# Layer 2's attention: how the mask reaches the transposed scores

## The chip, the cores and the metric

The kernel runs on one core of a Trainium2 chip. A core has a matrix engine (TensorE, "PE" in the profile, with its weight loads as "PEld"), a vector engine (VectorE, "DVE"), a scalar engine for functions such as the exponential (ScalarE, "ACT"), a general engine (GpSimd, "POOL") and a queue for transfers (SyncE, "SP"). Each works through its own queue in order, and they wait for one another by semaphores. Matrix products are written to PSUM, where the kernel keeps eight buffers (4, 3 and 1, by its pools) of 512 float32 numbers per partition, one bank each; everything else lies in SBUF.

The metric is the device time in microseconds of one execution.

## The reference

The program is four layers over `x` of shape (16, 128, 128), each with an attention or a product like one and a feed-forward part, both added through gates:

```python
x = x + tanh(g_xattn[2]) * _L2_xattn_ref(_layernorm(x), ctx, ctx, mask, Wq, bq, Wk, bk, Wv, bv, Wo, bo)
x = x + tanh(g_ffn[2]) * _L2_ffn_ref(...)
```

Layers 0, 1 and 3 have experts as feed-forward parts, layer 2 has slots. The attention of layer 2 has 16 heads of width 8 and one 128 by 128 mask for all sequences and heads:

```python
scores = einsum('bhqd,bhkd->bhqk', q, k) * scale
scores = where(mask == 0, -1e9, scores)
attn = softmax(scores, axis=-1)
out = einsum('bhqk,bhkd->bhqd', attn, v)
```

A query whose whole row of the mask is 0 gets equal weights over all keys.

## The kernel before

The 16 sequences are treated in four groups of four (`GB`), so a tile holds 128 partitions by 4 x 128 numbers, 512 in float32, which is one bank. For each group there is a chain: expert layer 1, attention of layer 2 (`attention_2(g)`), slots (`slots_2`), attention of layer 3 (`attention_3`), expert layer 3. The expert layers are one long generator, `experts()`, the stream: each of its steps is the products `pg` and `pu` (L452, L453), a function on ScalarE (L457), two products of elements on VectorE (`sg`, L458, and `h`, L464), the routing weight on GpSimd (`hw`, L473), and, two steps later (`LAG`), the product `acc` (L1128). `until(...)` at the end of the program draws the stream on as far as the next attention needs it, so that the stream's next group runs beside an attention.

The text is not the order of the engines' queues. When the program is built, a planner lays out one queue per engine by the place of the instructions in the text and by when their inputs are ready; `in_turn` adds edges that keep some of them in the written order. On the chip these queues are fixed.

`attention_2(g)` projects queries and keys with the heads laid out over partitions, then loops over the four sequences t of its group (L638 to L672). One iteration:

- Scores, queries on partitions: four banks `ps`, each started by a bfloat16 product of the identity with `mb`, a tile that holds -BIG (2 to the power 100) at masked places (L642), then 16 score products added (L647). L493, called at L650, takes the row maxima over the two heads of a half bank into `mp`.
- `mp` is transposed (L653) and added to the queries (L654): the product with the keys' tile `kTm` then gives scores less their maximum.
- Transposed scores, keys on partitions: again four banks, each started by a product with the identity, here of `mbT`, the mask transposed (L657), then 32 score products (L663).
- For i from 0 to 3: the exponential of bank i into an SBUF tile `pts` of 128 x 512 (L669, three buffers), and `weighted` (L495 to L503), which multiplies it with the values (L499) and with ones (L502) into `po`: weighted sums and sums of weights. These products stand in a fixed order.
- `over_weights`: reciprocal (L507) and product (L508) into `oT`.

The eight score banks of an iteration and `po` come from one pool of four buffers (`mm_tile`, and `acc_tile` while `side` is "m"). `attention_3(g)` has the same loop over pairs of sequences (L787 to L817) without any mask. `mask_i` is the mask loaded as integers; `maskf` is 0 at kept and -1 at masked places, and 0 all over in a row without a kept place; `someb` (0 or 1 for each query) takes out the queries of such a row. `LOWEST` is -3.0e38.

Of the kernel before, what the change touches and what calls it, by code (L numbers as in the profile page):

```python
# [10 lines left out]
F32 = mybir.dt.float32  # L11
BF16 = mybir.dt.bfloat16
I32 = mybir.dt.int32
AF = mybir.ActivationFunctionType
ALU = mybir.AluOpType
AX = mybir.AxisListType

P = 128
# [10 lines left out]
LOWEST = -3.0e38  # L29
BIG = 2.0**100  # L30
# [29 lines left out]
def flamingo(ctx, tc, x_in, ctx_in, mask_in, w1, w2, w3, wslot, wsmall, slots, cols_in, rows_in, consts_in,  # L60
             gu0, dn0, gu1, dn1, gu3, dn3, out):
    nc = tc.nc
    PSUM = bass.MemoryType.PSUM
    const = ctx.enter_context(tc.tile_pool(name="const", bufs=1))
# [23 lines left out]
    def mm_tile():  # L88
        return bank("mm")

    def tr_tile():
        return bank("tr")

    def acc_tile():
        return ps_acc.tile([P, CH], F32, tag="acc", name="acc") if side[0] != "m" else bank("po")

    def split(ap, n=GB):
        return ap.rearrange("p (t d) -> p t d", t=n)

    def bc(ap, axis, n):  # L100

        a = ap.unsqueeze(axis)
        shape = list(a.shape)
        shape[axis] = n
        return a.to_broadcast(shape)

    def mm(o, l, r, start=True, stop=True):
        nc.tensor.matmul(out=o, lhsT=l, rhs=r, start=start, stop=stop)  # L108
# [164 lines left out]
    def normed_T(g):  # L273
        xn = normed(g)
        return xn, transposed(xn, tag_of("xnT"), act, 2 if side[0] == "x" else 1)

    def add_gated(g, y, gate):
        nc.vector.scalar_tensor_tensor(X[g][:], y, gate, X[g][:], ALU.mult, ALU.add)

    def add_row(g, r):  # L280
        nc.gpsimd.tensor_tensor(X[g][:], X[g][:], bc(r[:], 1, GB), ALU.add)
# [9 lines left out]
    def keys_by_head(o, w, src, name, s):  # L291


        n = o.shape[2]
        p = mm_tile()
        mm(p[:, :n], w, src)
        for j in range(2):
            nc.vector.tensor_scalar(o[:, j, :], p[:, :n], con("hm")[:, j:j + 1], hcol[f"{name}{s}{j}"], ALU.mult, ALU.add)
# [140 lines left out]
    def in_turn(chain, ins):  # L439

        if chain:
            tc.add_manual_dep(ins.ins, chain[-1].name,
                              mybir.DependencyInfo(mybir.DependencyClass.NoSync, mybir.DependencyReason.DATA),
                              reason="in_turn")
        chain[:] = [ins.ins]
# [33 lines left out]
    def values(n, h0, nh, src, bias):  # L479

        o = vp[:, 0:n, 24:].rearrange("p t (h x) -> p t h x", h=NH)[:, :, h0:h0 + nh, 0:DK]
        shape = dict(t=n, h=nh)
        nc.vector.tensor_tensor(o, src.rearrange("p (t h d) -> p t h d", **shape),
                                bias.rearrange("p (t h d) -> p t h d", **shape), ALU.add)

    def value(rows, t, h):

        at = 24 + 32 * h - DK * (h % 4)
        return vp[rows, t, at:at + 32]

    def maxima(mp, i, src, n, k):

        nc.vector.tensor_reduce(mp[:, 0:n, 32 * i + 16:32 * i + 18], src, AX.X, ALU.max)  # L493

    def weighted(chain, heads, r, first, last):  # L495


        for po, jj, vcols, pts, rows in heads:
            in_turn(chain, nc.tensor.matmul(out=po[32 * jj:32 * jj + 32, 0, :], lhsT=vcols, rhs=pts, start=first, stop=last,  # L499
                                     skip_group_check=True))  # L500
        for po, jj, vcols, pts, rows in heads:
            in_turn(chain, nc.tensor.matmul(out=po[32 * jj:32 * jj + 32, 1, :], lhsT=own[rows, r, :], rhs=pts, start=False,  # L502
                                     stop=last, skip_group_check=True))  # L503

    def over_weights(o, po, n):
        rc = work.tile([P, P], F32, tag="rcw", name="rcw")
        nc.vector.reciprocal(rc[:, :n], po[:, 1, :])  # L507
        nc.vector.tensor_tensor(o, po[:, 0, :], rc[:, :n], ALU.mult)  # L508
# [113 lines left out]
    def attention_2(g):  # L622
        _, xnT = normed_T(g)
        add_row(g, ob2)
        qT = act.tile([P, 2, GT], F32, tag="qT", name="qT2")
        kTm = act.tile([P, 2, 2, GT], F32, tag="kTm", name="kTm2", bufs=1)
        for s in range(2):
            p = mm_tile()
            mm(p[:], W2H[:, s, :], xnT[:])
            nc.vector.scalar_tensor_tensor(split(qT[:, s, :]), split(p), hcol[f"bq2{s}"], bc(someb[:], 1, GB),  # L630
                                           ALU.add, ALU.mult)
            keys_by_head(kTm[:, s], W2H[:, 2 + s, :], CT[g][:], "bk2", s)
        pv = mm_tile()
        for t in range(GB):
            mm(pv[:, t * P:(t + 1) * P], CT[g][:, t * P:(t + 1) * P], w(W2, 0))
        values(GB, 0, NH, pv[:], bvr)
        oT = act.tile([P, GT], F32, tag="oT", name="oT2")
        for t in range(GB):  # L638
            b = slice(t * P, (t + 1) * P)
            ps = [mm_tile() for _ in range(4)]  # L640
            for i in range(4):
                nc.tensor.matmul(out=split(ps[i]), lhsT=identb[:], rhs=bc(mb[:], 1, 4), start=True, stop=False,  # L642
                                 skip_group_check=True)
            for s in range(2):
                for i in range(4):
                    rr = slice(32 * i, 32 * i + 32)
                    nc.tensor.matmul(out=split(ps[i])[:, 2 * s:2 * s + 2, :], lhsT=qT[rr, s, b], rhs=kTm[rr, s, :, b],  # L647
                                     start=False, stop=True, skip_group_check=True)
            for i in range(4):
                maxima(mp[:, 2 * t:2 * t + 2], i, ps[i][:].rearrange("p (s j k) -> p s j k", s=2, j=2), 2, P)  # L650
            pt = tr_tile()
            for s in range(2):
                nc.tensor.transpose(pt[:, s * P:(s + 1) * P], mp[:, 2 * t + s, :], ident[:])  # L653
            nc.vector.tensor_tensor(qT[:, :, b], pt[:, 0:2 * P].rearrange("p (s q) -> p s q", s=2), qT[:, :, b], ALU.add)  # L654
            ps = [mm_tile() for _ in range(4)]
            for i in range(4):
                nc.tensor.matmul(out=split(ps[i]), lhsT=identb[:], rhs=bc(mbT[:], 1, 4), start=True, stop=False,  # L657
                                 skip_group_check=True)
            for s in range(2):
                for j in range(2):  # L660
                    for i in range(4):
                        rr = slice(32 * i, 32 * i + 32)
                        nc.tensor.matmul(out=split(ps[i])[:, 2 * s + j, :], lhsT=kTm[rr, s, j, b], rhs=qT[rr, s, b],  # L663
                                         start=False, stop=True, skip_group_check=True)
            po = acc_tile()[:, 0:2 * P].rearrange("p (i q) -> p i q", i=2)
            chain = []
            for i in range(4):
                pts = work.tile([P, 4, P], F32, tag="pts", name="pts", bufs=3)
                nc.scalar.activation(pts[:], split(ps[i]), AF.Exp, scale=scale8)  # L669
                weighted(chain, [(po, jj, value(slice(0, P), t, 4 * jj + i), pts[:, jj, :], slice(0, P)) for jj in range(4)],  # L670
                         i, i == 0, i == 3)
            over_weights(oT[:, b], po, P)  # L672
        py = split(mm_tile())
        for t in range(GB):
            mm(py[:, t, :], oT[:, t * P:(t + 1) * P], w(W2, 1))
        add_gated(g, py, tgx[:, 2:3])
# [617 lines left out]
    pp = tr_tile()  # L1294
# [22 lines left out]
    pp = tr_tile()  # L1317
# [2 lines left out]
    nc.vector.tensor_copy(someb[:], pp[:, 0:P])  # L1320
    pp = tr_tile()
    nc.tensor.transpose(pp[:, 0:P], maskf[:], ident[:])
    mbT = const.tile([P, P], BF16, tag="mbT", name="mbT")
    nc.vector.tensor_scalar(mbT[:], pp[:, 0:P], BIG, None, ALU.mult)
    mb = const.tile([P, P], BF16, tag="mb", name="mb")
    nc.vector.tensor_scalar(mb[:], maskf[:], BIG, None, ALU.mult)
    identb = const.tile([P, P], BF16, tag="identb", name="identb")
# [11 lines left out]
    pp = mm_tile()  # L1339
# [3 lines left out]
    pp = mm_tile()  # L1343
# [3 lines left out]
    pp = tr_tile()  # L1347
# [3 lines left out]
    pp = mm_tile()  # L1351
# [24 lines left out]
    for g in range(NG + 1):  # L1376
        if g < NG:
            until(1, g)
            attention_2(g)
        if g > 0:  # L1380
            until("slots", g - 1)
            attention_3(g - 1)
# [78 lines left out]
```

## Time and profile before

Three runs took 898.25, 898.9 and 900.76 us: a median of 898.9.

| what | value |
|---|---|
| the profiled execution | 897.76 us |
| its span, first to last instruction | 896.1 us |
| granted TensorE clock, mean | 0.978 |
| products with `mbT` (L657) | 64, median 379 ns each |
| score products behind them (L663) | 512 instructions, median 270 ns |
| exponentials (L669) | 64, median 597 ns |
| maxima (L493) | 112, median 682 ns |
| `hw` on GpSimd (L473) | 142, median 1268 ns |

A busy time is the sum of the instructions' own times with overlaps taken once. TensorE's instructions are pipelined: one that is listed with 379 ns has its successor start long before it ends, so the cost of one in a row of many is the distance between starts. The iterations of `attention_2` lie in four stretches of the span, about 279 to 326, 351 to 402, 483 to 534 and 607 to 659 us, one for each group.

### The profile page before, as it was taken

Reading aid. Unit: us, or ns where it says so; the run is one execution under the profiler, and the core shown is the slowest. Engines: PE = TensorE matmul, PEld = TensorE weight load, DVE = VectorE, ACT = ScalarE, POOL = GpSimd, SP = SyncE. Lnnn points to the kernel's source line nnn. Section 1 sums busy time; section 2 is a strip of 40 time slices with the busy share of each in tenths; the row PEclk is TensorE's granted clock in tenths of the full one; section 3 lists DMA queues with packets and bytes.
Section 4 is the critical chain, followed back from the end, with each engine's and each line's share of the span. In section 5 each row is a group of like instructions: output and inputs, shape, how many; then the busy total and the mean of one; then the engine's idle time right before and its main releaser. Section 6 shows DMA issues by size and latency. Waiting matters only on the chain.

```text
span 896.1 us, 16095 instructions
## 1 busy us (share of the span) xinstructions
PE 824.0 (92%) x6189; PEld 465.0 (52%) x6189; DVE 570.6 (64%) x1600; ACT 262.6 (29%) x472; POOL 298.9 (33%) x310
## 2 busy tenths in 40 slices
PE   5899599888988999998999989999999999999997
PEld 4554499444444544554555554555555544554443
DVE  5774433467888467468677666768666678667522
ACT  2522255232331221322222222232222232222321
POOL 4447421576452122114321115311133122313443
PEclk9899599999999999999999999999999999999999
DMA  9451122741321011011111203110002111211230
GB/s 296 143 129 35 59 63 78 218 146 35 96 68 39 26 37 47 25 25 60 48 48 47 60 27 125 65 38 25 25 16 82 49 36 49 72 49 60 86 115 27
DMA packets 55677, 62.12 MB, mean 69 GB/s; under 512 B 14312, under 2 KB 33512, under 8 KB 55472
## 3 DMA queue, kind: packets, MB, share of 16 engines
q1 hardware_dynamic: 53536, 57.67, 21.1%
q0 software_dynamic: 1536, 3.15, 1.2%
q8 instruction: 49, 0.80, 0.4%
q10 hardware_dynamic: 528, 0.26, 0.1%
q14 instruction: 28, 0.23, 0.1%
HBM read 53.97 MB, written 7.09 MB: 68 GB/s over the span
## 4 chain that ended last, share of the span: by engine, by line
PE 49%; DVE 21%; POOL 11%; issue 10%; DMA 5%; ACT 3%; SPq 1%; POOLq 0%; DVEq 0%; ACTq 0%
PE mm L108 7%; POOL hw L473 6%; PE acc L1128 6%; PE pu L453 6%; PE pg L452 5%; PE po L499 3%; DVE h L464 3%; DVE sg L458 3%; DVE mp L493 3%; PE mm L647 2%; POOL xd L974 2%; PE po L502 2%; POOL rs L259 2%; PE pg L1069 2%; DMA cb<-combD 2%
## 5 line engine op out<-in xcount | busy, mean ns | idle before, releaser
L473 POOL TENSOR_TENSOR hw<-h,cb 128x512 f32<-128x512 f32 (+1 forms) x142 | 175.4, 1235 | 441.9 <-DVE h L464 357.8
L453 PE MATMUL pu<-xnTx,wall 128*128 128x512 f32 x288 | 152.0, 610 | 6.6 <-DVE sg L458 3.7
L452 PE MATMUL pg<-xnTx,wall 128*128 128x512 f32 x288 | 151.8, 609 | 1.1 <-ACT xnTx L243 0.7
L1128 PE MATMUL acc<-hw,wall 128*128 128x512 f32 x288 | 151.0, 608 | 0.6 <-POOL hw L473 0.5
L464 DVE TENSOR_TENSOR h<-sg,pu 128x512 f32<-128x512 f32 x147 | 100.7, 685 | 71.4 <-PE pu L453 58.9
L457 ACT ACTIVATE sg<-pg 128x512 f32<-128x512 f32 x105 | 62.8, 598 | 221.5 <-PE pg L452 219.9
L458 DVE SCALAR_TENSOR_TENSOR sg<-sg,pg 128x512 f32<-128x512 f32 x105 | 71.4, 680 | 32.8 <-ACT sg L457 32.7
L453 PEld LDWEIGHTS pu<-xnTx,wall 128*128 128x128 f32 x288 | 51.2, 190 | 65.8 <-issue 44.8
L1128 PEld LDWEIGHTS acc<-hw,wall 128*128 128x128 f32 x288 | 53.1, 193 | 56.2 <-issue 48.6
L493 DVE TENSOR_REDUCE mp<-mm 128x4 f32<-128x512 f32 (+1 forms) x112 | 65.8, 646 | 21.1 <-PE mm L647 19.9
L452 PEld LDWEIGHTS pg<-xnTx,wall 128*128 128x128 f32 x288 | 49.6, 192 | 40.6 <-issue 30.0
L507 DVE RECIPROCAL rcw<-po 128x128 f32<-128x128 f32 (+1 forms) x28 | 25.2, 900 | 52.8 <-PE po L502 45.0
L460 ACT ACTIVATE sg<-pg 128x512 f32<-128x512 f32 x51 | 30.4, 596 | 81.5 <-PE pg L452 81.4
L499 PE MATMUL po<-pts,vp 128*32 128x128 f32 (+1 forms) x896 | 45.9, 273 | 6.0 <-ACT pts L669 5.5
L259 POOL TENSOR_TENSOR rs<-ve,neghalf 128x4 f32<-128x4 f32 x32 | 32.8, 1025 | 55.6 <-DVE ve L257 53.5
L270 DVE TENSOR_SCALAR xn<-x,mv,rs 128x128 f32<-128x128 f32 x104 | 36.7, 410 | 20.9 <-POOL rs L259 20.9
L669 ACT ACTIVATE pts<-mm 128x512 f32<-128x512 f32 x64 | 33.8, 600 | 54.8 <-PE mm L663 54.4
L502 PE MATMUL po<-pts,own 128*32 128x128 f32 (+1 forms) x896 | 44.2, 265 | 0.0
L499 PEld LDWEIGHTS po<-pts,vp 128*32 128x32 f32 (+1 forms) x896 | 21.6, 108 | 28.8 <-ACT pts L669 14.3
L251 DVE BATCH_NORM_STATS2 st<-x 128x6 f32<-128x128 f32 x128 | 31.1, 305 | 8.3 <-DMA x<-in_x 7.7
L241 PE MATMUL tr<-ident,xn 128*128 128x128 f32 x100 | 23.1, 314 | 13.1 <-DVE xn L270 11.7
L647 PE MATMUL mm<-kTm,qT 32*128 32x256 f32 x256 | 30.4, 413 | 0.0
(355 smaller groups left out, 1234.9 us busy)
## 6 DMA issues: line engine op xcount, KB each, us to landing
cb<-combD SPq DMA_DIRECT2D x72, 256.0 KB, 3.3
cb<-combD SPq DMA_DIRECT2D x128, 128.0 KB, 2.8
wall<-in_gu SPq DMA_DIRECT2D x24, 256.0 KB, 4.4
wall<-in_dn SPq DMA_DIRECT2D x12, 256.0 KB, 5.5
xb<-xd SPq DMA_DIRECT2D x7, 256.0 KB, 3.1
yd<-yb SPq DMA_DIRECT2D x7, 256.0 KB, 2.3
xd<-vp SPq DMA_DIRECT2D x1, 1072.0 KB
x<-in_x SPq DMA_DIRECT2D x4, 256.0 KB, 4.9
```

What stands on the lines that cost most here:

```text
L108: nc.tensor.matmul(out=o, lhsT=l, rhs=r, start=start, stop=stop)
L259: latest["rs"] = nc.gpsimd.tensor_tensor(rs[:], ve[:], neghalf[:], ALU.pow).ins
L452: in_turn(chain, nc.tensor.matmul(out=pg[:], lhsT=w[:, 0], rhs=xnT[:], start=True, stop=True))
L453: in_turn(chain, nc.tensor.matmul(out=pu[:], lhsT=w[:, 1], rhs=xnT[:], start=True, stop=True))
L457: nc.scalar.activation(sg[:], pg[:], AF.Tanh, scale=0.5)
L458: nc.vector.scalar_tensor_tensor(sg[:], sg[:], 1.0, pg[:], ALU.add, ALU.mult)
L464: ins = nc.vector.tensor_tensor(h[:], sg[:], pu[:], ALU.mult)
L473: latest["hw"] = nc.gpsimd.tensor_tensor(hw[:, at:], h[:, at:], cb[:, at:], ALU.mult).ins
L493: nc.vector.tensor_reduce(mp[:, 0:n, 32 * i + 16:32 * i + 18], src, AX.X, ALU.max)
L499: in_turn(chain, nc.tensor.matmul(out=po[32 * jj:32 * jj + 32, 0, :], lhsT=vcols, rhs=pts, start=first, stop=last, skip_group_check=True))
L502: in_turn(chain, nc.tensor.matmul(out=po[32 * jj:32 * jj + 32, 1, :], lhsT=own[rows, r, :], rhs=pts, start=False, stop=last, skip_group_ch ...
L1128: in_turn(chain, nc.tensor.matmul(out=acc[0][:], lhsT=w[:, 2], rhs=h[:], start=n == 0, stop=last))
```

## The change

The transposed scores get no product with the mask any more: the score products L663 start their banks themselves. The mask comes in behind the exponential. A tile `keptT`, the transposed mask plus one, is 1 at kept and 0 at masked places, in float32. One instruction on VectorE per bank takes the smaller of the exponential and 3.0e38, since the exponential of a masked score, whose maximum was taken over kept places alone, may be infinite, and multiplies it with `keptT`, repeated over the four heads of the bank, in place. The first scores (L642) keep their products with `mb`.

```diff
             ps = [mm_tile() for _ in range(4)]
-            for i in range(4):
-                nc.tensor.matmul(out=split(ps[i]), lhsT=identb[:], rhs=bc(mbT[:], 1, 4), start=True, stop=False,
-                                 skip_group_check=True)
             for s in range(2):
                 for j in range(2):
                     for i in range(4):
                         rr = slice(32 * i, 32 * i + 32)
                         nc.tensor.matmul(out=split(ps[i])[:, 2 * s + j, :], lhsT=kTm[rr, s, j, b], rhs=qT[rr, s, b],
-                                         start=False, stop=True, skip_group_check=True)
+                                         start=True, stop=True)
...
                 pts = work.tile([P, 4, P], F32, tag="pts", name="pts", bufs=3)
+
                 nc.scalar.activation(pts[:], split(ps[i]), AF.Exp, scale=scale8)
+                nc.vector.scalar_tensor_tensor(pts[:], pts[:], -LOWEST, bc(keptT[:], 1, 4), ALU.min, ALU.mult)
                 weighted(chain, [(po, jj, value(slice(0, P), t, 4 * jj + i), pts[:, jj, :], slice(0, P)) for jj in range(4)],
                          i, i == 0, i == 3)
...
-    mbT = const.tile([P, P], BF16, tag="mbT", name="mbT")
-    nc.vector.tensor_scalar(mbT[:], pp[:, 0:P], BIG, None, ALU.mult)
+    keptT = const.tile([P, P], F32, tag="keptT", name="keptT")
+    nc.vector.tensor_scalar(keptT[:], pp[:, 0:P], 1.0, None, ALU.add)
```

## The prediction

> **What bounds the kernel now.** I read the page's busy row, then the chain that ended last, then the time line of layer 2's attention. The page first:
>
> ```profile
> PE 824.0 (92%) x6189; PEld 465.0 (52%) x6189; DVE 570.6 (64%) x1600; ACT 262.6 (29%) x472; POOL 298.9 (33%) x310
> ...
> PE 49%; DVE 21%; POOL 11%; issue 10%; DMA 5%; ACT 3%; SPq 1%; POOLq 0%; DVEq 0%; ACTq 0%
> ```
>
> TensorE is nearly full over the whole span, but the chain lies on it for only half of the time: at many places TensorE waits for VectorE. So the question is what the four stretches of layer 2's attention wait for. Their busy times (columns: stretch, length, then busy us and count of PE, PEld, DVE, ACT, POOL, and clock, DMA):
>
> ```profile
> 279.00:326.00 47.00, 44.75 (x530) 24.17 (x530) 27.95 (x57) 12.26 (x22) 7.39 (x6) 1.00 0.09 28
> 351.00:402.00 51.00, 48.63 (x557) 27.57 (x556) 28.81 (x66) 16.18 (x28) 5.12 (x5) 1.00 0.08 24
> 483.00:534.00 51.00, 47.52 (x566) 27.95 (x565) 34.98 (x109) 12.99 (x24) 6.27 (x6) 1.00 0.14 43
> 607.00:659.00 52.00, 48.78 (x564) 28.40 (x563) 34.82 (x108) 12.98 (x24) 6.28 (x6) 0.97 0.08 26
> ```
>
> Each holds four iterations over t, 10.5 us apart in group 0 (the reciprocals of L507 start at 292.52, 303.03, 313.55) and 11 to 12 us later on. One iteration, from the time line (start, length, engine, line, operation, count, idle before):
>
> ```profile
> 297.48 0.44 PE L653 MATMUL tr<-ident,mp 128*128 128x128 f32 x2 [0.26 <-DVE mp L493]
> ...
> 297.76 1.06 PE L657 MATMUL mm<-mbT,identb 128*128 128x512 bf16 x4
> 297.96 0.42 DVE L654 TENSOR_TENSOR qT<-tr,qT 128x256 f32<-128x256 f32 x1 [0.53 <-PE tr L653]
> ...
> 298.74 1.17 PE L663 MATMUL mm<-qT,kTm 32*128 32x128 f32 x32
> ...
> 299.99 2.28 ACT L669 ACTIVATE pts<-mm 128x512 f32<-128x512 f32 x4 [2.13 <-PE mm L663]
> ...
> 301.01 0.69 DVE L464 TENSOR_TENSOR h<-sg,pu 128x512 f32<-128x512 f32 x1 [2.03 <-PE pu L453]
> ...
> 301.77 1.28 POOL L473 TENSOR_TENSOR hw<-h,cb 128x512 f32<-128x512 f32 x1 [9.24 <-DVE h L464]
> ...
> 302.56 0.40 PE L502 MATMUL po<-pts,own 128*32 128x128 f32 x8
> ...
> 303.03 0.96 DVE L507 RECIPROCAL rcw<-po 128x128 f32<-128x128 f32 x1 [1.34 <-PE po L502]
> ```
>
> It is one serial chain: maxima, transposes (L653), q (L654), transposed scores (L663), exponentials (L669), weighted values (L499, L502), reciprocal, next scores. Four score banks plus `po` share four buffers, so the next iteration can't run far ahead. The expert stream fills TensorE's waits with only some three pieces (pg, pu, acc) per iteration: 5 `h` lie in group 0's stretch, 4 in each of the others. So what lengthens this chain lengthens the program, unless more expert pieces move in.
>
> **Part 1, the 64 products of L657 go.** Three of them take 0.81 us with the last one's 0.38 in it, so one starts every 0.215 us: 4 per iteration are 0.86 us of TensorE, 64 are 13.8 us. That is the ceiling. What of it lies on the chain? In six iterations (like the one above) the four stand together and partly cover the wait for q: L653 to L663 takes 1.26 us; without them q is ready 0.90 us after L653 starts (297.48 to 298.38), and L663 would start at about 0.97. Worth 0.29. In the other ten an expert piece stands between them:
>
> ```profile
> 490.13 0.44 PE L653 MATMUL tr<-ident,mp 128*128 128x128 f32 x2
> 490.40 0.81 PE L657 MATMUL mm<-mbT,identb 128*128 128x512 bf16 x3
> ...
> 491.05 1.02 PE L1128 MATMUL acc<-hw,wall 128*128 128x512 f32 x2
> ...
> 491.91 0.38 PE L657 MATMUL mm<-mbT,identb 128*128 128x512 bf16 x1
> ...
> 492.22 1.17 PE L663 MATMUL mm<-qT,kTm 32*128 32x128 f32 x32
> ```
>
> Here it takes 2.09. Layer 3's attention has the same loop without mask products, and shows what stays with one expert piece in the gap:
>
> ```profile
> 459.95 0.38 PE L799 MATMUL tr<-ident,mp 128*128 128x128 f32 x2
> 460.17 1.02 PE L452 MATMUL pg<-xnTx,wall 128*128 128x512 f32 x2
> ...
> 461.12 1.17 PE L808 MATMUL mm<-qT,kTm 32*128 32x128 f32 x32
> ```
>
> 1.17 to 1.23 us there (two places), so 0.88 is gained. Sum: 10 x 0.88 + 6 x 0.29 = 10.5 us off the chain.
>
> **Part 2, 64 multiplications on VectorE come in,** each between an exponential and its eight value products. Nearest rows for 128x512 f32: `sm<-se,rsum` (L380), both inputs in SBUF, 688 ns; `sg` (L458), the same opcode, 680 ns. I take 0.69. Back to back they start closer: four maxima of 0.68 take 2.48 us, so 0.60 apart, which the exponentials (0.56 apart) just keep up with. From the first exponential's start to the reciprocal it is 3.04 us now (299.99 to 303.03), 0.76 of it behind the last exponential. Then: 0.60 for the first exponential, 0.05 for the signal, 3 x 0.60 + 0.69 for the train, 0.76 behind it: 3.90, so 0.86 more. 16 x 0.86 = 13.8 us onto the chain. VectorE's load grows by 64 x 0.69 = 44 us, 11 us per stretch. Queued behind a waiting multiplication are the expert stream's sg and h, and TensorE's acc and GpSimd's hw wait for those; acc runs two expert steps behind (LAG), which covers one such delay.
>
> **Part 3, what else stands in VectorE's queue.** An `h` lies at 301.01, exactly inside the coming train; in groups 2 and 3 the slot routing and the expert routing (109 instructions instead of 57) lie there. Ends: nothing, if all of it goes before or after the train, and 0.60 in each of 16 iterations, 9.6 us, if one does not. Half, 4.8 us.
>
> **Part 4, the port.** The row: a multiply-add with its tensors all in SBUF,
>
> ```profile
> L1098 DVE SCALAR_TENSOR_TENSOR x<-y,by,x x24: 321/346/2027, 171.4 to 251.1; 128x128 f32<-128x128 f32 x24
> ```
>
> has a median of 346 ns, a maximum of 2027 and a mean of 503: some waited for over a microsecond. `sg` and `h`, which read one input from PSUM, show no such tail (means 680 and 685). The Trainium skill, page "SBUF — State Buffer", section "Who interferes with whom", says why this speaks against the change: a VectorE instruction with two SBUF inputs and a GpSimd one that reads SBUF exclude each other for the whole instruction. By that rule each iteration's hw (1.27 us, at 301.77 inside the coming train) costs up to 1.27: 16 x 1.27 = 20 us. By the row it is less: the mean wait was 503 - 346 = 0.16 us where GpSimd was busy 58.8 of 103 us (stretch 176 to 279); in attention's stretches it is busy 25 of 201. Scaled by that, 0.16 x 0.125 / 0.57 x 64 = 2.2 us. I take the row, 2.5 us; both ends (0 and 20) stay for the range.
>
> **Part 5, filling.** The wait for the first weights grows from 0.76 us to 1.34 (0.60 + 0.05 + 0.69), and six gaps at q have room for a piece of 0.86 at 0.23 of cost: 6 x 0.63 = 3.8 us of expert work comes inside. I take 4 off. That more comes in is the first rival. The mask tile itself is made once, one 128x128 instruction for another (0.28 us, L1324) far ahead of its use: nothing, or 0.3 us if that cover is gone.
>
> **Sum.** -10.5 + 13.8 + 4.8 + 2.5 - 4 = +6.6 us. The profiled execution took 897.8 us with a span of 896.1; the median of the runs is 898.9. All differences are made in the span; set on the median, 905.
>
> **The rivals.** *TensorE stays the bound (faster).* 92% busy speaks for it: all 13.8 us return, the next iteration's mask and score products (0.2 us pieces) fill the gaps between the value products, expert pieces the rest. If 16 x 0.35 us stays unfilled: -13.8 + 5.6 = -8, about 891. Against it: the stream now places one expert step per iteration although room for more was there. *VectorE becomes the bound (slower by much).* Groups 2 and 3 go from 35 to 46 us busy of 51. The densest long stretch before reached 79.0 of 103, or 77%. At that share the four stretches need 50.5, 51.5, 59.7 and 59.5 us where they have 47, 51, 51 and 52: +20, about 919. It decides once slot and routing instructions can't move out into the stretches between. *The two chains cancel.* 10.5 or 13.8 against 13.8 with queue and port hidden: 896 to 902.
>
> **Chances and range.** A measurement of this kernel can tell about 0.3%, 2.7 us, from no change. Forecast (902 to 912) 0.45; VectorE the bound 0.18; cancelled 0.13; TensorE the bound 0.24. So faster 0.24, same 0.13, slower 0.63. The range goes from the faster rival's centre to near the slow one's: 889 to 919; the likeliest case's own range is 901 to 912.
>
> **What would show it.** L657 gone and L653 to L663 at 1.0 to 1.25 us everywhere (part 1). The first exponential to the reciprocal at 3.9 us or more against 3.04 (part 2). Multiplications with a median of 690 ns and a tail over 1.2 us beside hw (part 4). TensorE's busy time down by about the 18 us that its row for L657 holds, its idle time up by more than its work went down. I am wrong if the iterations come closer than 10.5 us apart, or if more than 5 `h` lie in one stretch: then the stream filled what I call idle.

## The result and the profile after

The changed kernel takes 910.7 us (908.0 to 914.1) where the kernel before takes 898.9: a ratio of 1.0135, interval 1.0113 to 1.0157. It is 12 us slower; the forecast was 905, or 6 us slower. The profiled execution took 910.67 us, 12.9 more than the one before.

The page of the changed kernel, first its span and busy times, then from its groups of instructions the value products (L499), the new multiplications (L668) and the exponentials (now L667); behind the bar of each group stand its busy us, the mean ns of one, and the idle time just before it with what ended it:

```profile
span 908.9 us, 16012 instructions
...
PE 821.5 (90%) x6125; PEld 459.9 (51%) x6125; DVE 615.3 (68%) x1664; ACT 263.0 (29%) x472; POOL 300.6 (33%) x310
...
L499 PE MATMUL po<-pts,vp 128*32 128x128 f32 (+1 forms) x896 | 47.6, 283 | 19.0 <-DVE pts L668 18.5
...
L668 DVE SCALAR_TENSOR_TENSOR pts<-pts,keptT 128x512 f32<-128x512 f32 x64 | 45.9, 757 | 8.5 <-ACT pts L667 8.4
...
L667 ACT ACTIVATE pts<-mm 128x512 f32<-128x512 f32 x64 | 34.7, 596 | 36.2 <-PE mm L660 19.7 <-PE po L502 13.1 <-DVE pts L668 3.4
```

The rows of the value products and of the exponentials in the kernel before:

```profile
L499 PE MATMUL po<-pts,vp 128*32 128x128 f32 (+1 forms) x896 | 45.9, 273 | 6.0 <-ACT pts L669 5.5
...
L669 ACT ACTIVATE pts<-mm 128x512 f32<-128x512 f32 x64 | 33.8, 600 | 54.8 <-PE mm L663 54.4
```

TensorE has 64 products less, yet its busy time fell by only 2.5 us, and its idle time (span less busy) rose from 72.1 to 87.4. It now waits 19.0 us ahead of the value products, for VectorE, where the row before had 6.0, for ScalarE. VectorE has 44.7 us more. The last row after holds what the forecast did not have: exponentials waited 13.1 us for L502, the products that read an earlier exponential.

One iteration of group 0 after, from the time line, to be held against 299.99 to 303.03 of the kernel before:

```profile
285.65 1.17 PE L660 MATMUL mm<-qT,kTm 32*128 32x128 f32 x32
...
286.90 1.57 ACT L667 ACTIVATE pts<-mm 128x512 f32<-128x512 f32 x3 [0.55 <-PE mm L660]
287.53 1.90 DVE L668 SCALAR_TENSOR_TENSOR pts<-pts,keptT 128x512 f32<-128x512 f32 x3 [0.29 <-ACT pts L667]
...
288.99 0.60 ACT L667 ACTIVATE pts<-mm 128x512 f32<-128x512 f32 x1 [0.51 <-PE po L502]
...
289.94 0.68 DVE L668 SCALAR_TENSOR_TENSOR pts<-pts,keptT 128x512 f32<-128x512 f32 x1
...
291.52 0.96 DVE L507 RECIPROCAL rcw<-po 128x128 f32<-128x128 f32 x1 [0.89 <-PE po L502]
```

Three exponentials go out at once. The fourth starts only at 288.99, after L502 has read the first tile: `pts` has three buffers, and a tile is now held for a multiplication longer. From the first exponential to the reciprocal it is 4.62 us; before it was 3.04, and the forecast said 3.90.

The four stretches, as before by stretch, length, busy us of PE, PEld, DVE, ACT, POOL, then the clock and DMA:

```profile
275.00:329.00 54.00, 49.24 (x534) 25.58 (x533) 41.74 (x79) 12.89 (x24) 9.40 (x7) 1.00 0.10 33
354.00:408.00 54.00, 49.04 (x540) 27.08 (x539) 42.47 (x112) 17.12 (x29) 9.13 (x10) 1.00 0.10 30
484.00:545.00 61.00, 53.40 (x556) 29.43 (x554) 49.74 (x130) 15.14 (x28) 8.80 (x8) 0.94 0.15 40
616.00:676.00 60.00, 52.69 (x554) 29.70 (x553) 49.48 (x128) 14.87 (x27) 8.42 (x8) 0.94 0.07 19
```

VectorE is busy over 80% of the last two, and the granted clock there is 0.94. For comparisons I set the borders of a stretch alike in every kernel, from the first L642 of a group to the end of its last `oT`. All sums of this kind below are mine, from the profiled executions:

| kernel | four stretches | TensorE idle in them | `h` in them | the rest of the span |
|---|---|---|---|---|
| before | 195.3 | 11.3 | 17 | 700.8 |
| after | 227.4 | 24.6 | 22 | 681.5 |

The stretches grew by 32.1 us, and the rest of the span fell by 19.3: five more expert steps, and other work of routing and slots, now run inside the stretches. That is the whole difference of 12.8.

### The profile page after: what moved, and what is told of

Its sections match the earlier page's. It is cut to its first block, busy times and chain, and to the rows that moved or that the text cites. A ratio compares the mean times of both kernels' runs of the same rounds, so it can differ in the third digit from the quotient of the medians.

```text
span 908.9 us, 16012 instructions
## 1 busy us (share of the span) xinstructions
PE 821.5 (90%) x6125; PEld 459.9 (51%) x6125; DVE 615.3 (68%) x1664; ACT 263.0 (29%) x472; POOL 300.6 (33%) x310
## 5 line engine op out<-in xcount | busy, mean ns | idle before, releaser
L499 PE MATMUL po<-pts,vp 128*32 128x128 f32 (+1 forms) x896 | 47.6, 283 | 19.0 <-DVE pts L668 18.5
L668 DVE SCALAR_TENSOR_TENSOR pts<-pts,keptT 128x512 f32<-128x512 f32 x64 | 45.9, 757 | 8.5 <-ACT pts L667 8.4
L259 POOL TENSOR_TENSOR rs<-ve,neghalf 128x4 f32<-128x4 f32 x32 | 32.8, 1026 | 52.9 <-DVE ve L257 50.5
L499 PEld LDWEIGHTS po<-pts,vp 128*32 128x32 f32 (+1 forms) x896 | 21.4, 111 | 56.7 <-DVE pts L668 41.2
L270 DVE TENSOR_SCALAR xn<-x,mv,rs 128x128 f32<-128x128 f32 x104 | 34.7, 390 | 21.0 <-POOL rs L259 21.0
L507 DVE RECIPROCAL rcw<-po 128x128 f32<-128x128 f32 (+1 forms) x28 | 25.2, 900 | 32.2 <-PE po L502 22.8
L502 PE MATMUL po<-pts,own 128*32 128x128 f32 (+1 forms) x896 | 46.4, 276 | 0.6 <-issue 0.6
L667 ACT ACTIVATE pts<-mm 128x512 f32<-128x512 f32 x64 | 34.7, 596 | 36.2 <-PE mm L660 19.7
```

The costliest lines, as they stand in the source:

```text
L270: nc.vector.tensor_scalar(xn[:, t, :], x[:, t, :], mv[:, t, 0:1], rs[:, t:t + 1], ALU.subtract, ALU.mult)
L668: nc.vector.scalar_tensor_tensor(pts[:], pts[:], -LOWEST, bc(keptT[:], 1, 4), ALU.min, ALU.mult)
```

## The experiments

My theory: what costs is the longer chain from exponential to reciprocal, made of the train of multiplications, the ring of three `pts` tiles, and VectorE's queue and port; what the planner moves into the longer stretches gives a part back. The rivals: VectorE's load as such, and the port alone.

**The two halves of the change.** One kernel has neither products nor multiplications (it leaves out the mask of the transposed scores), the other has both. The first edit is shown against the changed kernel, the second against the kernel before:

```diff
-                nc.vector.scalar_tensor_tensor(pts[:], pts[:], -LOWEST, bc(keptT[:], 1, 4), ALU.min, ALU.mult)
```

> Leaves out the mask of the transposed scores altogether: neither the 64 products nor the 64 multiplications, so that masked keys get weight. What the removal alone gives. The forecast's part 1 (the gaps before the transposed scores shrink from 2.09 and 1.26 us): 10.5 us off 898.9, about 888. TensorE is the bound everywhere: all 13.8 us off, 885. The products were covered by other waits: within 2 us of 899.

```diff
+                nc.vector.scalar_tensor_tensor(pts[:], pts[:], -LOWEST, bc(keptT[:], 1, 4), ALU.min, ALU.mult)
...
+    keptT = const.tile([P, P], F32, tag="keptT", name="keptT")
+    nc.vector.tensor_scalar(keptT[:], pp[:, 0:P], 1.0, None, ALU.add)
```

> The kernel before with the 64 multiplications added behind the exponentials and the 64 products kept: what the addition alone costs. The trace of the changed kernel shows 4.6 to 4.9 us from the first exponential to the reciprocal in group 0 where it was 3.04, so if the chain sets the time: 16 x 1.6 = 26 us less a little that the expert stream fills, about 921. If the multiplications only matter as load of VectorE, and the products went for nothing: 911, as the changed kernel.

Without any: 891.4 us, ratio 0.9923 (0.9895 to 0.9951), so the removal alone is worth 4 to 9 us. With both: 913.9, ratio 1.0167 (1.0143 to 1.0190): the addition alone costs 13 to 17. The two add up to +0.9% (-0.8% and +1.7%), less than the +1.35% measured, though their intervals together reach it. The gain is neither nothing nor all 13.8 us of products. In the kernel without mask, group 2's first gap shows why:

```profile
485.07 0.44 PE L653 MATMUL tr<-ident,mp 128*128 128x128 f32 x2
485.35 1.02 PE L1126 MATMUL acc<-hw,wall 128*128 128x512 f32 x2
486.21 0.27 PE L241 MATMUL tr<-ident,xn 128*128 128x128 f32 x1
486.73 1.17 PE L660 MATMUL mm<-qT,kTm 32*128 32x128 f32 x32 [0.24 <-DVE qT L654]
```

It takes 1.66 us in place of 2.09, not 1.20: the scores now wait for q on VectorE, which the products had covered. Over 16 iterations the gap fell from 1.77 to 1.40 on average, 5.9 us.

**A fourth tile in the ring,** in both kernels. There was no room for it, so the reciprocal's two buffers became one, and one small tile (two in the changed kernel) took the place of a dead one; two controls have that room alone. The other users of this tile's place, layer 3's attention among them, have four as well.

```diff
-                pts = work.tile([P, 4, P], F32, tag="pts", name="pts", bufs=3)
+                pts = work.tile([P, 4, P], F32, tag="pts", name="pts", bufs=4)
...
-        rc = work.tile([P, P], F32, tag="rcw", name="rcw")
+        rc = work.tile([P, P], F32, tag="rcw", name="rcw", bufs=1)
```

> The changed kernel with four buffers for the exponentials in place of three (the room comes from tiles that are no longer in use and from one buffer less for the reciprocal). Theory of the ring: the fourth exponential now waits for the value products of the first bank, which wait for the first multiplication; without that wait the stretch from the first exponential to the reciprocal falls from 4.7 to the forecast's 3.9 us, 16 x 0.75 = 12 us off, 899 to 902. Theory of load (VectorE has 44 us more to do and is what sets the time): no change, 909 to 912.

> Control: the kernel before with the same four buffers and the same room made. There the fourth exponential started 1.7 us behind the first with no wait, so both theories expect no change: 897 to 901.

> Control: the changed kernel with three buffers, and only the room made as for four (one reciprocal buffer, two tiles in the place of others). If that room has no price: 909 to 912. If it is what cost the kernel before 6 us: 916, and the fourth buffer then gained 6.

> Control: the kernel before with three buffers and the room made. If the room has no price: 898 to 900, and the 6 us of the run with four buffers come from the fourth buffer's order of work and the clock (granted 0.969 there, 0.978 before). If it has: 905.

Changed kernel with four: 910.2, ratio 1.0123 (1.0101 to 1.0146); with the room alone: 913.4, ratio 1.0150 (1.0124 to 1.0176). Kernel before with four: 905.4 (1.0069); with the room alone: 905.7 (1.0076). So the room is what cost the kernel before its 6 us, and the fourth tile did nothing for its time. (The expectation was wrong that nothing waited there: in group 0 the fourth exponential starts 1.68 us behind the first with three tiles and 1.45 with four.) In the changed kernel it gained some 3 us, with intervals that overlap, and not the 12 that I expected. Yet the wait itself went, as the time line of the changed kernel with four tiles shows:

```profile
287.70 2.06 ACT L667 ACTIVATE pts<-mm 128x512 f32<-128x512 f32 x4 [0.49 <-PE mm L660]
288.33 2.50 DVE L668 SCALAR_TENSOR_TENSOR pts<-pts,keptT 128x512 f32<-128x512 f32 x4 [0.23 <-ACT pts L667]
...
291.59 0.96 DVE L507 RECIPROCAL rcw<-po 128x128 f32<-128x128 f32 x1 [0.17 <-PE po L502]
```

All four go at once, and the reciprocal comes 3.89 us after the first exponential: the forecast's 3.90, which had been worked out without the ring. Over all sixteen iterations the time from exponential to reciprocal fell from 90.3 us (room alone) to 82.2, and the gaps before the scores fell by 2.5. Yet the stretches fell only from 225.6 to 223.1 us, and the rest of the span grew by 1.8. What was gained in the chain was lost again elsewhere in the iterations, and the clock may be part of it: inside the four stretches TensorE had half clock for 20.5 us with four tiles and for 10.2 with the room alone, which by an estimate (half of the difference) is up to 5 us. So the 3 us are what the fourth tile brought, and not the price of the ring by itself. That freeing the ring alone returns the loss is refuted.

**Exponentials in PSUM.** This takes ring and port away together: the exponential goes back into its score bank, and the multiplication has one input in SBUF.

```diff
-                nc.scalar.activation(pts[:], split(ps[i]), AF.Exp, scale=scale8)
-                nc.vector.scalar_tensor_tensor(pts[:], pts[:], -LOWEST, bc(keptT[:], 1, 4), ALU.min, ALU.mult)
+                nc.scalar.activation(split(ps[i]), split(ps[i]), AF.Exp, scale=scale8)
+                nc.vector.scalar_tensor_tensor(pts[:], split(ps[i]), -LOWEST, bc(keptT[:], 1, 4), ALU.min, ALU.mult)
```

> The changed kernel, but the exponential is written back into its score bank in PSUM, and the multiplication reads it there and writes the SBUF tile. The multiplication then has one input in SBUF, and the fourth exponential needs no free SBUF tile. Theory of ring and port: first exponential to reciprocal 3.9 us in group 0, multiplications at 690 ns with no tail (mean 757 in the changed kernel), 16 x 0.75 + 4 = up to 16 us off the chain, 900 to 906. Theory of load (VectorE's 44 us more): no change, 909 to 912. A price against it: banks come free one multiplication later, which could cost the next iteration's scores up to 0.7 us each, then 911 or more.

> As the run with exponentials in PSUM, with four SBUF tiles as well. Ring: nothing is left to gain by the fourth tile there, so as that run within 3 us, unless four tiles carry a price of their own, as the kernel before showed with them (905.4 for 899.1): then 6 us above it.

897.6 us, ratio 0.9982 (0.9970 to 0.9995): the whole loss is gone, with the same 64 multiplications on VectorE. In group 0 all four exponentials go at once, and the reciprocal comes 4.00 us after the first:

```profile
289.78 2.05 ACT L667 ACTIVATE mm<-mm 128x512 f32<-128x512 f32 x4 [0.54 <-PE mm L660]
...
293.78 0.96 DVE L507 RECIPROCAL rcw<-po 128x128 f32<-128x128 f32 x1 [0.31 <-PE po L502]
```

The stretches take 215.5 us and hold 22 `h` as the changed kernel's do, and the rest of the span is 680.4, near the 681.5 there. So the 12 us came out of the stretches, and they lie in the chain: from exponential to reciprocal the sixteen iterations take 80.7 us in all, 12.7 less than the changed kernel's 93.4. Of these, 3.3 us lie in the first iteration of group 1 (7.32 us there, 4.00 here), where the queue of ScalarE in the changed kernel has two loads of function tables between the third and the fourth exponential; here they stand behind the fourth. With four tiles too: 899.4 (1.0009), nothing more to gain. VectorE's 44 us of load as such can't be what makes the changed kernel slower than this one: they are all still there. Against the kernel without any mask (ratio 0.9923) the multiplications still cost some 5 us.

**The port alone.** Exponentials in SBUF and three tiles, but the second input in PSUM (the mask is left out, and the larger of exponential and score is taken):

```diff
-                nc.vector.scalar_tensor_tensor(pts[:], pts[:], -LOWEST, bc(keptT[:], 1, 4), ALU.min, ALU.mult)
+                nc.vector.scalar_tensor_tensor(pts[:], pts[:], -LOWEST, split(ps[i]), ALU.min, ALU.max)
```

> The changed kernel with the exponentials in SBUF and three buffers as there, but the second input of the instruction behind each exponential is the score bank in PSUM in place of the mask tile, and the larger of the two is taken: the mask is left out, and the weights are others. What it tells is the port alone: one input in SBUF, while the ring of three stays. If the port is most of the 13 us that exponentials in PSUM gave back: 899 to 903, and no instruction of it above 0.7 us. If the ring is: 908 to 911, with 4.6 us from the first exponential to the reciprocal in group 0. If each does half, 904 to 907.

The instruction by its line, min, median and max in ns, in the changed kernel and then in this one:

```profile
L668 DVE SCALAR_TENSOR_TENSOR pts<-pts,keptT x64: 675/684/1616, 287.5 to 671.6; 128x512 f32<-128x512 f32 x64
```

```profile
L668 DVE SCALAR_TENSOR_TENSOR pts<-pts,mm x64: 677/681/690, 289.3 to 671.0; 128x512 f32<-128x512 f32 x64
```

The tail is gone and the time is not: 911.0, ratio 1.0150 (1.0129 to 1.0171). Taking the port away brought nothing here. It did not come quite alone, though: in group 0 the time from exponential to reciprocal is now 4.5 to 5.8 us, and not the expected 4.6. The ring alone gave 3 us and the port alone none, yet the kernel without both is 13 us faster; that each hides behind the other fits this, but I have not shown it. Exponentials in PSUM change the planner's order too, as the table loads show, and what that is worth was not tested.

**Mixtures.** Multiplications from PSUM for the first banks, products for the last ones:

```diff
-            for i in range(4):
+            for i in range(2, 4):
...
+                to = split(ps[i]) if i < 2 else pts[:]
+                nc.scalar.activation(to, split(ps[i]), AF.Exp, scale=scale8)
+                if i < 2:
+                    nc.vector.scalar_tensor_tensor(pts[:], to, -LOWEST, bc(keptT[:], 1, 4), ALU.min, ALU.mult)
```

> A mixture: banks 0 and 1 masked by multiplications read from PSUM, banks 2 and 3 by products with the identity as before. By the chain: first exponential to reciprocal 3.1 us (as before, since the last banks' exponentials set it), two products of 0.43 us in the wait for q, most of it covered: 891 to 895, below both kernels. By TensorE's work: 6.9 us less than before, the same range. By VectorE's load (22 us more): 905.

> As the mixture, with only bank 3 masked by a product: first exponential to reciprocal 3.4 us, three multiplications per iteration. By the chain 893 to 896, between the mixture of two and the run with all exponentials in PSUM (897.6). By load 908.

Both missed. Two products: 899.7 (1.0005, interval 0.9993 to 1.0017), with 3.55 us from exponential to reciprocal in group 0 and not 3.1. One product: 905.4 (1.0076), above both its neighbours. With 0, 2, 3 and 4 multiplications from PSUM per iteration the kernel takes 898.1, 899.7, 905.4 and 897.6 us: no order that load or TensorE's work would make. The stretches, though, follow the chain: from exponential to reciprocal the mean is 3.35, 4.42, 5.25 and 5.04 us, and the four stretches take 195.3, 207.4, 221.4 and 215.5. It is the rest of the span that goes the other way, 700.8, 690.8, 681.6 and 680.4, as longer stretches take in more. So the forecasts by the chain missed twice: the chain itself was longer than forecast, and what moves in is not part of it.

**Load without the place in the chain.** The kernel before, with 64 instructions that nobody reads:

```diff
+                nc.vector.scalar_tensor_tensor(aside[:], split(ps[i]), 1.0, bc(ones[:], 1, 4), ALU.mult, ALU.mult)
```

> The kernel before with all its products, and 64 instructions of the same size on VectorE that read the score banks and write a tile that nobody reads: the load without the place in the chain (one input in SBUF, no wait behind it except for the bank). By the theory of load: 908 to 912, like the changed kernel. By chain and port: 899 to 903; what is above 899 is what queueing on VectorE alone costs.

915.1, ratio 1.0201 (1.0172 to 1.0230). It seems to speak for load, but the experiment did not separate what it was meant to. The value products waited for the instruction aside after all:

```profile
290.39 1.49 DVE L670 SCALAR_TENSOR_TENSOR aside<-mm,ones 128x512 bf16<-128x512 f32 x2 [0.67 <-ACT pts L669]
...
291.13 0.43 PE L499 MATMUL po<-pts,vp 128*32 128x128 f32 x8 [0.40 <-DVE aside L670]
...
293.78 0.95 DVE L507 RECIPROCAL rcw<-po 128x128 f32<-128x128 f32 x1
```

`po` takes the bank of the first scores, and the instruction aside still reads that bank. From the first exponential (289.76) to the reciprocal it is 4.02 us, a chain 0.98 longer in group 0 and 1.7 longer on the mean of all sixteen iterations. So the run shows another wait at the same place, and leaves pure load open.

## Why the forecast held, and where it didn't

The direction and the place were right: the gap ahead of the transposed scores shrank, the train on VectorE cost more, and the wait of TensorE moved from the exponential to the multiplication. The size was half of the measured one, and the terms were further off than their sum:

| term of the forecast | forecast | from the traces |
|---|---|---|
| products gone, L653 to the scores | -10.5 | -3.5 (mean 1.77 to 1.55) |
| train, in iterations with no other wait | +13.8 | +13.6 (16 x (3.89 - 3.04), with four tiles) |
| ring of three tiles | none | +11.7 (16 x (4.62 - 3.89)) |
| queue and port | +7.3 | +14.5 (what is left) |
| more work inside | -4.0 | -19.3, and -4.2 elsewhere in the iterations |
| sum | +6.6 | +12.8 |

What was measured is the gap, the time from the first exponential to the reciprocal (its mean rose from 3.35 to 5.84 us, 39.8 us in all), the stretches (32.1, which is 39.8 - 3.5 - 4.2) and the rest of the span. The split of the 39.8 is an estimate: train and ring (25.3) are the first iteration of group 0 taken sixteen times, and queue and port are what is left. Over all sixteen iterations the fourth tile took 8.1 us off this time, not 11.7.

- *Part 1 was mis-sized.* For the ten iterations with an expert piece in the gap I took that of layer 3's attention, 1.2 us, and for the other six 0.97. None came below 1.17: an expert piece moved into those too. Group 0 has 1.17 to 1.23. In groups 2 and 3 the scores came 1.65 to 2.07 us after the transposes in six of eight, since q, or another expert piece, was late. My sign for this part, TensorE's busy time down by some 18 us, failed as well: it fell by 2.5, as the records of other products cover more time than before, those of the first scores (L642, L647) 6.7 us and those of L499 and L502 3.9.
- *Part 2 was right for the train and left out the ring.* The forecast let all four exponentials start at once; the first iteration of the trace with three tiles shows the fourth held back. The 0.56 us that I took for the pace of the exponentials was already a sign of it, since with four tiles they start 0.48 apart. As a term of the chain the ring comes to 8 to 12 us, though taking it away returned only about 3.
- *Part 3 was too small in groups 2 and 3.* In their first two iterations it takes 7.1 to 7.9 us from exponential to reciprocal, with the routing's small instructions ahead of and between the multiplications: the first exponential of one starts at 507.39, the first multiplication at 510.44.

```profile
507.39 1.57 ACT L667 ACTIVATE pts<-mm 128x512 f32<-128x512 f32 x3 [0.49 <-PE mm L660]
507.71 0.36 DVE L352 MAX8 m<-gs 128x8 f32<-128x8 f32 x4
...
509.90 0.47 DVE L352 MAX8 m<-m 128x8 f32<-128x32 f32 x4
...
510.44 1.88 DVE L668 SCALAR_TENSOR_TENSOR pts<-pts,keptT 128x512 f32<-128x512 f32 x3
```

- *Part 4 by the row was near.* The waits at the port come to 64 x (757 - 684 ns) = 4.7 us, against 2.5 from the row and 20 from the rule of the Trainium skill (page "SBUF — State Buffer", "Who interferes with whom") applied to every iteration. The rule agrees with the trace: the seven multiplications that took more than 1.2 us, up to 0.93 more than the median, all lie beside an `hw` that had begun first. It didn't cost as much, since few trains meet an `hw`, and the wait can fall on the other side: in the kernel with both maskings four `hw` began while a multiplication ran, took 1.64 to 1.65 us in place of 1.27, and no multiplication took more than 694 ns. Where the tail was taken away no time came back.
- *Part 5 was far too small,* and my own sign of being wrong, more than 5 `h` in a stretch, came true: 6, 6, 5 and 5. The rival with VectorE as the bound had three of the four stretches right within 1 us, 50.5, 51.5, 59.7 and 59.5 us for a measured 51.3, 55.4, 60.6 and 60.0. It missed the total, 919, since the rest of the span fell by 19.3.

So 905 for 910.7 was a sum of errors that partly cancelled: the direction came from the mechanism, and that the sum came so near was luck. Without the mask at all the kernel gains some 8 us; the multiplications, as the change has them, cost some 15.

## What to carry to other kernels

Where an instruction is put between a producer and its consumer, count the buffers between them, not the durations alone: a tile is held longer by the new instruction, and with one buffer fewer than there are steps the last step waits for the first. If the new instruction can read its input where the producer's own input lies (here the score bank in PSUM), neither the ring nor the shared port is touched, and here the same multiplications then cost no more than the products did: 897.6 us, 0.2% below the kernel before, no more than a draw. Where a planner lays out the queues, a stretch that gets longer takes in other work, so a sum over the chain must say what comes in; and a control is needed for the side effects of an edit, since the room made for a fourth tile (one buffer less for the reciprocal, one tile in the place of another) moved the kernel before by 0.8%.

## What the runs showed of the hardware

The granted clock fell where TensorE waits longest. Before, the stretches of groups 0 to 2 ran at 1.00 and that of group 3 at 0.97; after, the stretches of groups 2 and 3 each have two spans of 3.4 us at half clock, mean 0.94. Each of the four begins in a wait of TensorE for the multiplications, of 2.04 or 2.75 us, or at most 1.7 us behind it. Weighed over the span, (1 - 0.975) x 910.7 = 22.8 us of clock are missing after, and 19.8 before, so at most 3 of the 12 us. The four runs of the changed kernel follow their clock: 908.0 us at 0.977, 910.7 and 910.8 at 0.975, 914.1 at 0.972. The Trainium skill, page "TensorE: Matmul & The Clock Gate", section "What's actually happening", has half clock after at least one idle window of about 3.4 us. The length of the spans agrees; the waits in these stretches were shorter than that, 2.75 us at most, so a single wait of that length is not what this trace shows, and what decided stays open. With a fourth tile there was more half clock inside the stretches each time: 20.5 us for 10.2 in the changed kernel, 13.7 for 6.8 in the kernel before (both against the room alone), 17.1 for 6.8 with exponentials in PSUM. Why is not shown.

An exponential that ScalarE wrote back into PSUM, and a multiplication that read it there, took no longer than in SBUF: the four exponentials start to end 2.05 us (2.06 in SBUF), the multiplication has a mean of 684 ns with a maximum of 694.
